# The start of a transformer block on one core: condition turned first, filler matmuls on ones, the first normalised rows on two engines

## The chip, the cores and the metric

The kernel runs on one core of a Trainium2 chip. The core has a matrix engine (TensorE, PE in the profile; its weight loads are listed as PEld), a vector engine (VectorE, DVE), a scalar engine (ScalarE, ACT), a general engine (GpSimd, POOL) and SyncE (SP), which here only issues DMAs. The metric is the device time of one execution in microseconds (us). Three runs of the kernel before took 1156.21, 1156.73 and 1157.76 us; the median is 1156.73.

## The reference

Input is x, 2 batches of 1024 tokens of width 256, one condition vector of 256 for each batch, and 77 context tokens for each batch. All weights are float32. Cut to what matters:

```python
x = x + xcond(layernorm(x), cond, ctx)
x = x + ffn(layernorm(x))              # a small network with rounded weights

def xcond(x, t, context):              # 16 heads of 64
    h1 = layernorm(x) * (1 + scale1) + shift1   # scale, shift = split(t @ norm1_w + norm1_b)
    x = mha(h1, h1) + x
    h2 = layernorm(x) * (1 + scale2) + shift2
    x = mha(h2, context) + x
    h3 = layernorm(x) * (1 + scale3) + shift3
    return glu_ff(h3) + x
```

Only the beginning concerns us: the double layer norm of the first batch's tokens, the first pair of scale and shift, and the first projections to keys and queries.

## The kernel before

All 2048 tokens lie in SBUF as 16 tiles of 128 tokens (`r_sb`). Self-attention goes unit by unit: a unit is a pair of heads with one half (512) of a batch's queries, and there are 32. A unit has 4 slots; in each slot (the loop at L1102) PE makes two groups of scores, ACT copies them out of PSUM, DVE keeps a running maximum, and the exponentials, sums on POOL and products with the values of an earlier unit are worked in between. Projections, values and other pieces are hung onto slots in three dictionaries (`pieces`, `inner`, `extras`). The order on PE, DVE, ACT and POOL in this part is the order in which the program is written, and each of these engines works strictly through its own list; a later part of the kernel is ordered by a planner, which the change doesn't touch.

Ahead of the slots stands a start of its own, written out in L1063 to L1089. PE has no weights yet. It turns the identity matrix 23 times as filler (L1066), and then turns `vec`, 32 rows of short vectors that ACT's queue has loaded: the shift vectors of three norms, the bias of the feed-forward part and the condition. ACT copies the result to `vecT` (L1068), and POOL adds one to the scale parts (L1071). DVE works out mean and variance for four tiles (`first_stats`: `bn_stats` and `bn_aggr` for each tile, then two operations on the variances), ACT takes a square root, DVE a reciprocal. The normalised rows `xn` of the first four tiles are made half by ACT, half by DVE (`first_xn`). PE multiplies condition and weights (`shift_scale_flat`), DVE copies the flat result, PE turns it into columns (`shift_scale`), and DVE adds the bias into `scsh`. `first_turned` transposes `xn` to PSUM, column half by column half, and `first_T` scales and shifts it on ACT into `h1T`, the transposed input of the projections. After that come the same steps for tiles 4 to 7, with the first halves of the k and q projections (`project`) between them, and the slots begin. `first_y` writes the normalised tokens back on POOL, which isn't waited for soon.

PSUM is handed out by tags. `two_banks` rotates two buffers of two banks, mainly for scores; `piece_bank` is one bank, `maxima_banks` a pair of banks for the broadcast maxima, which have no use for it until the second unit, and the tag `av` one bank for the products with the values. Whoever asks for a buffer waits until the readers of its last holder are done. Slot 0 has, behind its scores, the k projection of the second half of the tokens, in the maxima's banks (L1029), and slot 1 the q projection (L1030).

Loads are issued by SP in the order of L338 to L352; the queue also waits for older transfers to land.

Of the kernel before, what the change touches and what calls it, by code (L numbers as in the profile page):

```python
# [26 lines left out]
P = 128  # L27
# [16 lines left out]
def block_kernel(ctx: ExitStack, tc: tile.TileContext, a: dict, out: bass.AP):  # L44
# [20 lines left out]
    xv = a["x"].rearrange("b (t p) d -> p (b t) d", p=P)  # L65
    ident = const.tile([P, P], FP, name="ident")
# [3 lines left out]
    ones = const.tile([P, P], FP, name="ones")  # L70
    nc.gpsimd.memset(ones, 1.0)
# [194 lines left out]
    with ExitStack() as sa:  # L266
# [49 lines left out]
        for n in range(3):  # L316
            nc.scalar.dma_start(
                out=vec[4 * n : 4 * n + 4, :],
                in_=g(f"xcond_norm{n + 1}_b").rearrange("(o p) -> o p", p=P),
            )  # L320
        for c in range(DC):
            nc.scalar.dma_start(
                out=vec[28 + B * c : 28 + B * (c + 1), :],
                in_=a["cond_1024"][:, c * P : (c + 1) * P],
            )
        nc.scalar.dma_start(
            out=vec[12:28, :], in_=g("xcond_ff_b1").rearrange("(o p) -> o p", p=P)
        )
# [4 lines left out]
        def load_nw(n):  # L333
            nc.sync.dma_start(
                out=nw[n], in_=g(f"xcond_norm{n + 1}_w").rearrange("(c p) f -> p c f", p=P)
            )
# [3 lines left out]
        load_nw(0)  # L340
        load_pair(0)
        load_x(4, 4)
# [3 lines left out]
        load_pair(1)  # L346
        bo1 = load_row("xcond_attn1_bo", D)
# [218 lines left out]
        h1T, mvs, rws, xns, pts = {}, {}, {}, {}, {}  # L566

        def first_stats(b, half):
            st = small.tile([P, 4, 6], FP, tag="st4", name="st")
            mv = mvs[b, half] = p1.tile([P, 4, 2], FP, tag="mv4", name="mv", bufs=4)  # L570
            rw = rws[b, half] = p1.tile([P, 3, 4], FP, tag="rw4", name="rw", bufs=4)
            for i in range(4):
                nc.vector.bn_stats(st[:, i, :], r_sb[:, b * TB + 4 * half + i, :])
                nc.vector.bn_aggr(mv[:, i, :], st[:, i, :])
            nc.vector.tensor_scalar(rw[:, 0, :], mv[:, :, 1], 1.0 + EPS, EPS * EPS, ALU.mult, ALU.add)
            nc.vector.tensor_scalar_add(rw[:, 1, :], mv[:, :, 1], EPS)
# [16 lines left out]
        def first_xn(b, half, on_act=0):  # L593
# [4 lines left out]
            for i in range(4):  # L598
                src = r_sb[:, b * TB + 4 * half + i, :]
                if i < on_act:  # L600
                    nc.scalar.activation(
                        xn[:, i, :], src, AF.Identity,
                        bias=rw[:, 2, i : i + 1], scale=rw[:, 0, i : i + 1],
                    )
                else:
                    normed(xn[:, i, :], src, mv, rw[:, 0, :], i)

        def first_turned(b, half, parts=range(DC)):
            if b not in h1T:
                h1T[b] = hpool.tile([P, DC, S], FP, tag="hT", name=f"h1T_{b}")  # L610
            if 0 in parts:
                pts[b, half] = (maxima_banks if b else two_banks)("pt_ln")
            pt = pts[b, half]
            for c in parts:
                for i in range(4):
                    at = c * 512 + i * P
                    nc.tensor.transpose(
                        pt[:, at : at + P], xns[b, half][:, i, c * P : (c + 1) * P], ident
                    )

        def first_T(b, half):
            pt = pts.pop((b, half))
            for c in range(DC):
                nc.scalar.activation(  # L624
                    h1T[b][:, c, half * 512 : (half + 1) * 512],
                    pt[:, c * 512 : (c + 1) * 512],
                    AF.Identity,
                    bias=scsh[:, 0, 1, c, b : b + 1],
                    scale=scsh[:, 0, 0, c, b : b + 1],
                )  # L630
# [11 lines left out]
        def shift_scale_flat(n):  # L642

            pf = psx.tile([P, 512], FP, tag="av", name="pf")
            for c in range(DC):
                nc.tensor.matmul(
                    pf[:B, :],
                    lhsT=vecT[:, 28 + B * c : 28 + B * (c + 1)],
# [4 lines left out]
            if n:  # L653
                nc.scalar.copy(flat, pf[:B, :])
            else:
                nc.vector.tensor_copy(flat, pf[:B, :])

        def shift_scale(n):
# [8 lines left out]
            if n == 0:  # L667
                nc.vector.tensor_tensor(
                    scsh[:, n, :, :, :].rearrange("p s c b -> p (s c) b"),
                    pe[:, : 4 * B].rearrange("p (o b) -> p o b", b=B),  # L670
                    vecT[:, 4 * n : 4 * n + 4].unsqueeze(2).to_broadcast([P, 4, B]),
# [3 lines left out]
            for oc in range(4):  # L675
                nc.scalar.activation(
                    scsh[:, n, oc // DC, oc % DC, :], pe[:, oc * B : (oc + 1) * B], AF.Identity,
                    bias=vecT[:, 4 * n + oc : 4 * n + oc + 1],
# [383 lines left out]
        at_slot(extras, 112, load_u, 0)  # L1062
        first_stats(0, 0)  # L1063
        pv = piece_bank("pv")
        for i in range(23):
            nc.tensor.transpose(pv[:, P : 2 * P], ident, ident)  # L1066
        nc.tensor.transpose(pv[:, :NV], vec, ident[:NV, :NV])
        nc.scalar.copy(vecT, pv[:, :NV])  # L1068
        for n in range(3):
            v = vecT[:, 4 * n : 4 * n + DC]  # L1070
            nc.gpsimd.tensor_scalar_add(v, v, 1.0)  # L1071
        first_sqrt(0, 0)
        first_inverse(0, 0)
        first_xn(0, 0, 2)
        first_y(0, 0)
        shift_scale_flat(0)
        first_turned(0, 0, (0,))
        shift_scale(0)
        first_turned(0, 0, (1,))
        first_T(0, 0)  # L1080
        first_stats(0, 1)
# [4 lines left out]
        project(0, 0, "q", 0, two_banks)  # L1086
# [419 lines left out]
    with (  # L1506
# [338 lines left out]
        class Piece:  # L1845
# [25 lines left out]
            def gelu(self, f):  # L1871
# [4 lines left out]
                    bias=vecT[:, 20 + f : 21 + f],  # L1876
                )

            def gate(self, f):
                n = self.n * P  # L1880
                nc.vector.scalar_tensor_tensor(  # L1881
                    self.gT[:, f, :n], self.pu[f][:, :n], vecT[:, 12 + f : 13 + f],
# [93 lines left out]
```

## Time and profile before

| what | us |
|---|---|
| median of three runs | 1156.73 |
| the profiled execution | 1156.76 |
| its span in the trace | 1155.0 |
| PE busy | 1132.8 |
| DVE busy | 922.1 |
| POOL busy | 848.3 |
| ACT busy | 815.5 |
| first filler transpose begins | 1.45 |
| `vecT` is copied | 6.88 |
| first projection begins | 12.54 |
| second half's k projection begins | 19.85 |

The span runs from the first to the last instruction of the trace. The time of an execution is 1.76 us longer. In the lines shown below, a group of instructions has its line in the program, engine, operation, written and read tiles, the count after x, and times in us from the start of the span. "L365 PE MATMUL pp<-h1T,wk" is the projection to keys, whose helper has line 365. In the chain of work, each line is a start, a duration and what ran; in the groups, busy time and mean nanoseconds stand behind the first bar, idle time ahead of it and who ended it behind the second.

### The profile page before, as it was taken

The numbers are of one execution on the slowest core, as the hardware profiler recorded it, in microseconds if no ns is written. First come the engines' busy times: TensorE is split into PE (matmuls) and PEld (weight loads), VectorE is DVE, ScalarE is ACT, GpSimd is POOL, SyncE is SP. The second block draws the span as 40 slices with busy tenths as digits, with TensorE's granted clock in tenths as the row PEclk, the third lists the DMA queues.
The fourth block names the chain that finished last, engine by engine and source line by source line (L and its number), as shares of the span: only waits on it lengthen the run. The fifth ranks groups of instructions, "written<-read, shape, count | busy, mean of one in ns | idle before, by whom it ended". The sixth has DMA issues, their size and how long they took to land.

```text
span 1155.0 us, 18728 instructions
## 1 busy us (share of the span) xinstructions
PE 1132.8 (98%) x6964; PEld 531.9 (46%) x6964; DVE 922.1 (80%) x1319; ACT 815.5 (71%) x1023; POOL 848.3 (73%) x654
## 2 busy tenths in 40 slices
PE   8999999999999999999999999999999999999997
PEld 4333333333333333333333333355677866486685
DVE  5898889879888988989987899977767634587497
ACT  4788887888887888888889888765544231665366
POOL 5688989888888788888988899979765424424145
PEclk9999999999999999999999999999999999999999
DMA  7011212212122121211113212121201020000000
GB/s 242 25 33 56 72 60 67 69 50 81 48 74 61 57 79 38 85 51 61 56 40 103 95 38 83 34 92 43 82 1 74 1 82 19 1 19 10 10 10 29
DMA packets 65041, 64.32 MB, mean 56 GB/s; under 512 B 23675, under 2 KB 54709, under 8 KB 64309
## 3 DMA queue, kind: packets, MB, share of 16 engines
q1 hardware_dynamic: 64885, 63.10, 17.5%
q8 instruction: 55, 0.90, 0.3%
q14 instruction: 37, 0.30, 0.1%
q10 hardware_dynamic: 64, 0.02, 0.0%
HBM read 55.36 MB, written 7.73 MB: 55 GB/s over the span
## 4 chain that ended last, share of the span: by engine, by line
PE 82%; DVE 10%; ACT 5%; issue 2%; POOL 1%; DVEq 0%; ACTq 0%; POOLq 0%
PE sc L432 17%; PE pav L506 16%; PE pu L1863 10%; PE pp L365 9%; PE po L948 6%; PE po L1889 5%; PE sc L859 4%; PE pv L365 4%; PE po L365 3%; DVE macc L448 3%; DVE sT L488 3%; ACT sT L1107 2%; ACT sT L491 2%; PE tot L529 1%; POOL pacc L498 1%
## 5 line engine op out<-in xcount | busy, mean ns | idle before, releaser
L498 POOL TENSOR_TENSOR pacc<-pacc,sT 128x1024 f32<-128x1024 f32 x192 | 457.1, 2381 | 25.8 <-ACT sT L491 15.5
L448 DVE TENSOR_TENSOR macc<-macc,sc 128x1024 f32<-128x1024 f32 x192 | 233.8, 1218 | 71.1 <-ACT sT L1107 59.5
L1107 ACT COPY sT<-sc 128x1024 f32<-128x1024 f32 x256 | 248.0, 1017 | 51.8 <-PE sc L432 51.6
L491 ACT ACTIVATE sT<-sT 128x1024 f32<-128x1024 f32 x256 | 260.1, 1064 | 13.3 <-DVE sT L488 11.8
L488 DVE TENSOR_TENSOR sT<-sT,mb 128x1024 f32<-128x1024 f32 x224 | 260.0, 1205 | 3.5 <-ACT mb L479 3.4
L432 PE MATMUL sc<-qT,kT 64*64 64x512 f32 x2048 | 252.9, 604 | 3.4 <-DVE macc L448 1.9
L506 PE MATMUL pav<-sT,v 128*64 128x512 f32 x1024 | 248.5, 605 | 2.9 <-ACT sT L491 2.4
L506 PEld LDWEIGHTS pav<-sT,v 128*64 128x64 f32 x1024 | 61.6, 136 | 160.0 <-issue 72.0
L432 PEld LDWEIGHTS sc<-qT,kT 64*64 64x64 f32 x2048 | 62.7, 131 | 150.1 <-issue 59.8
L498 POOL TENSOR_TENSOR pacc<-sT 128x1024 f32<-128x1024 f32 x32 | 76.3, 2384 | 67.0 <-ACT sT L491 66.9
L1863 PE MATMUL pu<-h2T,ffw 128*128 128x512 f32 (+1 forms) x320 | 114.0, 508 | 0.0
L1863 PEld LDWEIGHTS pu<-h2T,ffw 128*128 128x128 f32 x320 | 59.7, 190 | 44.8 <-issue 41.1
L484 POOL TENSOR_TENSOR sT<-sT,wide 128x1024 f32<-128x1024 f32 x32 | 76.2, 2380 | 1.7 <-DMA wide<-md 1.7
L859 PE MATMUL sc<-h1T,G 128*128 128x512 f32 x160 | 72.0, 602 | 0.0
L948 PE MATMUL po<-U,p 128*128 128x256 f32 x320 | 71.4, 380 | 0.0
L1881 DVE SCALAR_TENSOR_TENSOR gT<-pu,vecT,ge 128x512 f32<-128x512 f32 (+1 forms) x40 | 25.7, 641 | 50.2 <-ACT ge L1874 50.1
L948 PEld LDWEIGHTS po<-U,p 128*128 128x128 f32 x320 | 59.9, 190 | 8.0 <-issue 0.2
L365 PE MATMUL pv<-wv,h1T 128*64 128x256 f32 x512 | 61.8, 379 | 0.0
L365 PE MATMUL po<-wo,aT 128*64 128x256 f32 x512 | 61.5, 380 | 0.3 <-POOL aT L562 0.3
L365 PE MATMUL pp<-h1T,wk 128*64 128x512 f32 x256 | 60.6, 594 | 0.9 <-ACT h1T L624 0.9
L365 PE MATMUL pp<-h1T,wq 128*64 128x512 f32 x256 | 60.5, 593 | 0.0
L1874 ACT ACTIVATE ge<-pu,vecT 128x512 f32<-128x512 f32 (+1 forms) x40 | 23.9, 598 | 50.0 <-PE pu L1863 50.0
(195 smaller groups left out, 1491.6 us busy)
## 6 DMA issues: line engine op xcount, KB each, us to landing
wide<-md SPq DMA_DIRECT2D x32, 512.0 KB
rinv<-td SPq DMA_DIRECT2D x64, 128.0 KB
ffw<-in_L_xcond_ff_w_dram SPq DMA_DIRECT2D x3, 1024.0 KB
gd<-cw SPq DMA_DIRECT2D x32, 80.0 KB
ud<-cw SPq DMA_DIRECT2D x32, 80.0 KB
U<-ud SPq DMA_DIRECT2D x2, 1280.0 KB
wk<-in_L_xcond_attn_wk_dram SPq DMA_DIRECT2D x16, 128.0 KB
wq<-in_L_xcond_attn_wq_dram SPq DMA_DIRECT2D x16, 128.0 KB
```

The lines of the kernel that those rows point to most:

```text
L365: nc.tensor.matmul(dst[half, :], lhsT=lhsT[:, half], rhs=rhs, start=start, stop=stop)
L432: nc.tensor.matmul(sc[cols, j * 512 : (j + 1) * 512], lhsT=kTs[b, pair][rows, kb * P + c * DH : kb * P + (c + 1) * DH], rhs=qTs[b, pair][r ...
L448: nc.vector.tensor_tensor(maccs[u], old, sc, ALU.max)
L484: nc.gpsimd.tensor_tensor(t, t, wides[u], ALU.subtract)
L488: nc.vector.tensor_tensor(sT[u, kb], sT[u, kb], mbs[u], ALU.subtract)
L491: nc.scalar.activation(sT[u, kb], sT[u, kb], AF.Exp)
L498: nc.gpsimd.tensor_tensor(paccs[u], old, sT[u, kb], ALU.add)
L506: nc.tensor.matmul(pavs[u][j * DH : (j + 1) * DH, :], lhsT=vs[b, pair // 2][:, kb, at : at + DH], rhs=sT[u, kb][:, j * 512 : (j + 1) * 512 ...
L859: nc.tensor.matmul(sc[:, j * 512 : (j + 1) * 512], lhsT=Gs[self.b][c][:, 2 * k + j, :], rhs=hT[:, c, self.at : self.at + 512], start=(c == 0),
L948: nc.tensor.matmul(self.po[i][:, :D], lhsT=self.t[piece // 2][:, at : at + P], rhs=Us[self.b][:, piece, :], start=(piece == 0), stop=(piec ...
L1107: nc.scalar.copy(sT[v, kb], sc)
L1863: nc.tensor.matmul(pu[:, k * 512 : k * 512 + n], lhsT=ffw1[c][:, at : at + P], rhs=hT[:, c, at0 : at0 + n], start=(c == 0), stop=(c == DC ...
```

## The change

The vectors in `vec` change places: the condition comes first, then the shift vectors, then the feed-forward bias. Only the condition and the first shift vector are loaded by ACT's queue; the others go to SP's, behind the second pair of projection weights. The first 8 rows are turned and copied alone, the other 24 in slot 1 (`later_vectors`). The weights of the first scale and shift are loaded in two pieces, and tiles 4 to 7 in two. The tile of ones is filled by DVE instead of POOL, at the head of the program.

The 23 transposes of the identity become 15 matmuls of ones (128 x 128) with 64 columns of ones, the turning of 8 vectors, and 8 more such matmuls, into a pair of banks of `two_banks`. The product of condition and weights moves ahead of the normalised rows, its copy from DVE to ACT. All four tiles of `xn` are made by DVE. The eight transposes go tile by tile, two tiles to each of two PSUM buffers, and `first_T` reads one buffer on ACT and the other on DVE. The moments of tiles 4 and 5 are taken between `xn` and `scsh`, those of 6 and 7 after `first_T`. The second half's transposes take the maxima's banks instead of `two_banks`, and the first q projection the bank of tag `av`.

```diff
...
     r_sb = const.tile([P, NT, D], FP, name="r_sb")
     xv = a["x"].rearrange("b (t p) d -> p (b t) d", p=P)
+    ones = const.tile([P, P], FP, name="ones")
+    nc.vector.memset(ones, 1.0)
     ident = const.tile([P, P], FP, name="ident")
     make_identity(nc, ident)
     ident_bf = const.tile([P, P], BF, name="ident_bf")
     nc.vector.tensor_copy(ident_bf, ident)
-    ones = const.tile([P, P], FP, name="ones")
-    nc.gpsimd.memset(ones, 1.0)
     NV = 32
     vecT = const.tile([P, NV], FP, name="vecT")
     scsh = const.tile([P, 3, 2, DC, B], FP, name="scsh")
...
         nw12 = w8.tile([P, 2, DC, 2 * D], FP, tag="aT", name="nw12")
         nw = [nw0, nw12[:, 0, :, :], nw12[:, 1, :, :]]
         ctx_sb = w8.tile([CTX, B, D], FP, tag="aT", name="ctx_sb")
-        for n in range(3):
-            nc.scalar.dma_start(
-                out=vec[4 * n : 4 * n + 4, :],
-                in_=g(f"xcond_norm{n + 1}_b").rearrange("(o p) -> o p", p=P),
-            )
         for c in range(DC):
             nc.scalar.dma_start(
-                out=vec[28 + B * c : 28 + B * (c + 1), :],
-                in_=a["cond_1024"][:, c * P : (c + 1) * P],
-            )
-        nc.scalar.dma_start(
-            out=vec[12:28, :], in_=g("xcond_ff_b1").rearrange("(o p) -> o p", p=P)
-        )
+                out=vec[B * c : B * (c + 1), :], in_=a["cond_1024"][:, c * P : (c + 1) * P]
+            )
+
+        def load_shift(n, queue):
+            queue.dma_start(
+                out=vec[4 + 4 * n : 8 + 4 * n, :],
+                in_=g(f"xcond_norm{n + 1}_b").rearrange("(o p) -> o p", p=P),
+            )
+
+        load_shift(0, nc.scalar)
         def load_x(t, n):
             nc.sync.dma_start(out=r_sb[:, t : t + n, :], in_=xv[:, t : t + n, :])
-        def load_nw(n):
+        def load_nw(n, parts=slice(0, DC)):
             nc.sync.dma_start(
-                out=nw[n], in_=g(f"xcond_norm{n + 1}_w").rearrange("(c p) f -> p c f", p=P)
+                out=nw[n][:, parts, :],
+                in_=g(f"xcond_norm{n + 1}_w").rearrange("(c p) f -> p c f", p=P)[:, parts, :],
             )
         load_x(0, 2)
         load_x(2, 2)
-        load_nw(0)
+        for c in range(DC):
+            load_nw(0, slice(c, c + 1))
+        load_x(4, 2)
         load_pair(0)
-        load_x(4, 4)
+        load_x(6, 2)
         load_wv(0)
         load_x(8, 4)
         load_x(12, 4)
         load_pair(1)
+        load_shift(1, nc.sync)
+        load_shift(2, nc.sync)
+        nc.sync.dma_start(
+            out=vec[16:NV, :], in_=g("xcond_ff_b1").rearrange("(o p) -> o p", p=P)
+        )
         bo1 = load_row("xcond_attn1_bo", D)
         load_nw(1)
         load_nw(2)
...
-        h1T, mvs, rws, xns, pts = {}, {}, {}, {}, {}
+        h1T, sts, mvs, rws, xns, pts = {}, {}, {}, {}, {}, {}
         def first_stats(b, half):
-            st = small.tile([P, 4, 6], FP, tag="st4", name="st")
-            mv = mvs[b, half] = p1.tile([P, 4, 2], FP, tag="mv4", name="mv", bufs=4)
-            rw = rws[b, half] = p1.tile([P, 3, 4], FP, tag="rw4", name="rw", bufs=4)
-            for i in range(4):
+            first_moments(b, half, range(4))
+            first_variances(b, half)
+
+        def first_moments(b, half, rows):
+            if 0 in rows:
+                sts[b, half] = small.tile([P, 4, 6], FP, tag="st4", name="st")
+                mvs[b, half] = p1.tile([P, 4, 2], FP, tag="mv4", name="mv", bufs=4)
+            st, mv = sts[b, half], mvs[b, half]
+            for i in rows:
                 nc.vector.bn_stats(st[:, i, :], r_sb[:, b * TB + 4 * half + i, :])
                 nc.vector.bn_aggr(mv[:, i, :], st[:, i, :])
+
+        def first_variances(b, half):
+            mv = mvs[b, half]
+            rw = rws[b, half] = p1.tile([P, 3, 4], FP, tag="rw4", name="rw", bufs=4)
             nc.vector.tensor_scalar(rw[:, 0, :], mv[:, :, 1], 1.0 + EPS, EPS * EPS, ALU.mult, ALU.add)
             nc.vector.tensor_scalar_add(rw[:, 1, :], mv[:, :, 1], EPS)
...
                 rw[:, 2, :], mv[:, :, 0], -1.0, rw[:, 0, :], ALU.mult, ALU.mult
             )
-        def first_xn(b, half, on_act=0):
+        def first_xn(b, half):
             xn = xns[b, half] = p3.tile([P, 1024], FP, tag="sT", name="xn").rearrange(
                 "p (i d) -> p i d", d=D
             )
             mv, rw = mvs[b, half], rws[b, half]
             for i in range(4):
                 src = r_sb[:, b * TB + 4 * half + i, :]
-                if i < on_act:
-                    nc.scalar.activation(
-                        xn[:, i, :], src, AF.Identity,
-                        bias=rw[:, 2, i : i + 1], scale=rw[:, 0, i : i + 1],
-                    )
-                else:
-                    normed(xn[:, i, :], src, mv, rw[:, 0, :], i)
+                normed(xn[:, i, :], src, mv, rw[:, 0, :], i)
         def first_turned(b, half, parts=range(DC)):
             if b not in h1T:
                 h1T[b] = hpool.tile([P, DC, S], FP, tag="hT", name=f"h1T_{b}")
             if 0 in parts:
-                pts[b, half] = (maxima_banks if b else two_banks)("pt_ln")
+                if b or half:
+                    pts[b, half] = [maxima_banks("pt_ln").rearrange("p (c n) -> p c n", c=DC)]
+                else:
+                    pts[b, half] = [
+                        two_banks("pt_ln")[:, :512].rearrange("p (c n) -> p c n", c=DC)
+                        for _ in range(2)
+                    ]
             pt = pts[b, half]
-            for c in parts:
-                for i in range(4):
-                    at = c * 512 + i * P
+            each = 4 // len(pt)
+            for i in range(4):
+                for c in parts:
                     nc.tensor.transpose(
-                        pt[:, at : at + P], xns[b, half][:, i, c * P : (c + 1) * P], ident
+                        pt[i // each][:, c, i % each * P : (i % each + 1) * P],
+                        xns[b, half][:, i, c * P : (c + 1) * P],
+                        ident,
                     )
         def first_T(b, half):
-            pt = pts.pop((b, half))
             for c in range(DC):
-                nc.scalar.activation(
-                    h1T[b][:, c, half * 512 : (half + 1) * 512],
-                    pt[:, c * 512 : (c + 1) * 512],
-                    AF.Identity,
-                    bias=scsh[:, 0, 1, c, b : b + 1],
-                    scale=scsh[:, 0, 0, c, b : b + 1],
-                )
+                for at, pt in enumerate(pts[b, half]):
+                    n = pt.shape[2]
+                    out = h1T[b][:, c, half * 512 + at * n : half * 512 + (at + 1) * n]
+                    bias, scale = scsh[:, 0, 1, c, b : b + 1], scsh[:, 0, 0, c, b : b + 1]
+                    if at:
+                        nc.vector.tensor_scalar(out, pt[:, c, :], scale, bias, ALU.mult, ALU.add)
+                    else:
+                        nc.scalar.activation(out, pt[:, c, :], AF.Identity, bias=bias, scale=scale)
         def first_y(b, half):
             for i in range(4):
...
             for c in range(DC):
                 nc.tensor.matmul(
                     pf[:B, :],
-                    lhsT=vecT[:, 28 + B * c : 28 + B * (c + 1)],
+                    lhsT=vecT[:, B * c : B * (c + 1)],
                     rhs=nw[n][:, c, :],
                     start=(c == 0),
                     stop=(c == DC - 1),
                 )
-            if n:
-                nc.scalar.copy(flat, pf[:B, :])
-            else:
-                nc.vector.tensor_copy(flat, pf[:B, :])
-
-        def shift_scale(n):
+            nc.scalar.copy(flat, pf[:B, :])
+
+        def shift_scale(n, meanwhile=lambda: None):
             pe = psx.tile([P, 512], FP, tag="av", name="pe")
             for oc in range(4):
...
                     ident[:B, :B],
                 )
             if n == 0:
+                meanwhile()
                 nc.vector.tensor_tensor(
                     scsh[:, n, :, :, :].rearrange("p s c b -> p (s c) b"),
                     pe[:, : 4 * B].rearrange("p (o b) -> p o b", b=B),
-                    vecT[:, 4 * n : 4 * n + 4].unsqueeze(2).to_broadcast([P, 4, B]),
+                    vecT[:, 4 + 4 * n : 8 + 4 * n].unsqueeze(2).to_broadcast([P, 4, B]),
                     ALU.add,
                 )
                 return
             for oc in range(4):
                 nc.scalar.activation(
                     scsh[:, n, oc // DC, oc % DC, :], pe[:, oc * B : (oc + 1) * B], AF.Identity,
-                    bias=vecT[:, 4 * n + oc : 4 * n + oc + 1],
+                    bias=vecT[:, 4 + 4 * n + oc : 5 + 4 * n + oc],
                 )
...
             at_slot(inner, 98 + 12 * half, norm_half, 1, 0, half)
         at_slot(extras, 112, load_g, 0)
         at_slot(extras, 112, load_u, 0)
+
+        def idle(times):
+            for _ in range(times):
+                nc.tensor.matmul(
+                    spare[:, :DH], lhsT=ones, rhs=ones[:, :DH], start=True, stop=True
+                )
+
+        def vectors_turned(bank, lo, hi):
+            nc.tensor.transpose(bank[:, :hi], vec[:hi, :], ident[:hi, :hi])
+            nc.scalar.copy(vecT[:, lo:hi], bank[:, lo:hi])
+            for n in range(3):
+                if lo <= 4 + 4 * n < hi:
+                    v = vecT[:, 4 + 4 * n : 4 + 4 * n + DC]
+                    nc.gpsimd.tensor_scalar_add(v, v, 1.0)
+
+        def later_vectors():
+            vectors_turned(psx.tile([P, 512], FP, tag="av", name="pv2"), 8, NV)
+
+        at_slot(inner, 1, later_vectors)
         first_stats(0, 0)
-        pv = piece_bank("pv")
-        for i in range(23):
-            nc.tensor.transpose(pv[:, P : 2 * P], ident, ident)
-        nc.tensor.transpose(pv[:, :NV], vec, ident[:NV, :NV])
-        nc.scalar.copy(vecT, pv[:, :NV])
-        for n in range(3):
-            v = vecT[:, 4 * n : 4 * n + DC]
-            nc.gpsimd.tensor_scalar_add(v, v, 1.0)
+        pv, spare = piece_bank("pv"), two_banks("spare")
+        idle(15)
+        vectors_turned(pv, 0, 8)
+        idle(8)
         first_sqrt(0, 0)
         first_inverse(0, 0)
-        first_xn(0, 0, 2)
+        shift_scale_flat(0)
+        first_xn(0, 0)
         first_y(0, 0)
-        shift_scale_flat(0)
-        first_turned(0, 0, (0,))
-        shift_scale(0)
-        first_turned(0, 0, (1,))
+        first_turned(0, 0)
+        shift_scale(0, lambda: first_moments(0, 1, (0, 1)))
         first_T(0, 0)
-        first_stats(0, 1)
+        first_moments(0, 1, (2, 3))
+        first_variances(0, 1)
         first_root(0, 1)
         first_xn(0, 1)
         first_y(0, 1)
         project(0, 0, "k", 0)
-        project(0, 0, "q", 0, two_banks)
+        project(0, 0, "q", 0, lambda name: psx.tile([P, 512], FP, tag="av", name=name))
         first_turned(0, 1)
         first_T(0, 1)
         add_row(0, TB, bo1)
...
```

In the hunk left out at the end, the feed-forward part reads its bias from the new columns of `vecT`.

## The prediction

> **What bounds the kernel now.** I read the page first: its engine table and the row of forty slices.
>
> ```profile
> PE 1132.8 (98%) x6964; PEld 531.9 (46%) x6964; DVE 922.1 (80%) x1319; ACT 815.5 (71%) x1023; POOL 848.3 (73%) x654
> ...
> PE   8999999999999999999999999999999999999997
> ```
>
> TensorE (PE) works through 39 of the 40 slices at 90% or more; only the first, 29 us long, and the last have room. The change touches only the first. After about 20 us PE has no gaps worth the name (the table of short stretches has it busy 2.00 of each 2.00 us from 20 to 30 us), so what counts is how early that unbroken stretch starts. I take its start to be the k projection of the second half of the tokens. The chain of work in order of time shows what stands ahead of it:
>
> ```profile
> 1.45 5.17 PE pv L1066 x23
> 6.62 0.24 PE pv L1067
> ...
> 7.09 1.28 ACT L584
> 8.37 0.01 issue
> 8.38 0.22 ACT rw L584
> ...
> 9.06 1.10 ACT xn L601 x2
> ...
> 11.71 0.79 ACT h1T L624
> 12.50 0.04 issue
> 12.54 3.65 PE pp L365 x16
> 16.20 1.04 PE pt_ln L617 x8
> 17.23 0.02 issue
> 17.26 1.46 ACT h1T L624 x2
> 18.71 0.04 issue
> 18.76 1.09 PE sc L432 x8
> 19.85 1.87 PE pp L365 x8
> ```
>
> So the start of the kernel hangs on the 23 filler transposes. The turned vectors come behind them, the copy of these stands ahead of the square root on ScalarE (ACT), and a table load of 1.28 us stands between copy and square root. The statistics had been ready since 6.0 us. Call E the end of the fillers: 6.41 us (in the timeline the last one starts at 6.20, and they run 0.21 apart). The DVE normalisations begin at 8.94, E + 2.53. The projections begin at P0 = 12.54, E + 6.13. The unbroken stretch begins at 19.85, P0 + 7.31.
>
> **The filler: what one costs now.** Three answers carry this: the instructions on the filler's tile, the groups of weight loads by shape, and a close look at the one place where matmuls with 128 stationary columns and almost nothing to stream follow each other.
>
> ```profile
> L1066 PE MATMUL pv<-ident x23: 421/421/477, 1.5 to 6.2; 128*128 128x128 f32 x23
> 16.13 0.86 PEld L617 LDWEIGHTS pt_ln<-ident,xn 128*128 128x128 f32 x8 [0.81 <-issue]
> L1426 PEld LDWEIGHTS pm<-wpart,ones 128*128 128x128 f32 x4 | 0.6, 191 | 0.1
> L365 PEld LDWEIGHTS pp<-h1T,wk 128*64 128x64 f32 x256 | 18.0, 137 | 37.2 <-issue 31.4 <-ACT sT L1107 3.0 <-ACT h1T L624 1.6
> L529 PEld LDWEIGHTS tot<-pacc,ones 128*32 128x32 f32 x256 | 5.0, 108 | 20.8 <-ACT sT L491 16.8 <-issue 2.1 <-POOL pacc L498 1.9
> 915.58 0.36 PE L1426 MATMUL pm<-wpart,ones 128*128 128x1 f32 x2
> 915.69 0.25 PE L1426 MATMUL pm<-wpart,ones 128*128 128x1 f32 x1
> ```
>
> 22 steps between 1.5 and 6.2 make 0.213 us per filler transpose; the same transpose at 16 us takes 0.107 (0.86 over 8). So PE ran at half speed to the end of the fillers. The first product on real weights starts at 7.12 and its four instructions take 1.88 us, exactly as those at 29.86 do, so the full clock came between 6.4 and 7.1 us, 5.0 to 5.7 us after PE's first instruction. The view's granted clock reads 1.00 throughout and does not show this. In float32 a matmul is two instructions, each with its own weight load (L1426 has four for two matmuls). The loads take 108, 137 and 191 ns for 32, 64 and 128 columns, some 0.107 us more for 128 columns than for none, and the ones that stream a single column start 0.11 us apart: there the load is the bound. One `idle` matmul loads 128 columns twice and streams 64 twice. I price it by those loads: 2 x 0.107 at full clock, 2 x 0.213 at half, twice a filler transpose of now. The other bound is the stream alone (a half of the transpose's 128 columns, twice): 0.213 at half clock. I take the loads, since L1426 has the same 128 x 128 stationary shape.
>
> **The change, part by part.** *Ones on DVE, first.* PE need no longer wait for the identity (1.41). The queues start at 0.71; POOL's fill of the same tile took 0.21; so PE starts near 0.97 instead of 1.45. If DVE is later than that, each 0.1 costs 0.1.
>
> *15 idle matmuls, then 8 vectors turned.* 30 passes from 0.97, half speed up to the time x at which the clock is released: E' = 0.97 + 30 x 0.107 + (x - 0.97)/2 = 3.69 + x/2, at most 7.37. With the delay seen now (middle 5.3 us) x = 6.3 and E' = 6.82, later than the 6.41 of now. Bounds: 4.17 (streams alone at half clock) and 7.37 (cold throughout). The Trainium skill, "TensorE: Matmul & The Clock Gate", Part 1, puts the release at 3.4 to 4 us of sustained work with a phase that isn't tied to the kernel; by it x would be 4.4 to 5.0, E' 5.9 to 6.2 and the gain below 1.2 to 0.9. Its Part 4 says that transposes don't count as work for the release, which would speak strongly for this change; the trace disagrees, since nothing but transposes came before the fast products at 7.12.
>
> *From there to the normalised rows.* The copy (8 columns instead of 32: 0.19 at most), the table load, the square root, the reciprocal and the product stay in the same order on ACT and DVE: first row E' + 2.53. All four rows go to DVE (1.46 for four, as at 14.64), so to E' + 3.99 where now two and two end at E + 3.74: 0.25 lost, and the transposes, now row by row, end at E' + 4.4. They no longer end last.
>
> *8 idle matmuls and the condition's product.* 16 passes at full clock, 1.71, from E' + 0.35; the product to E' + 3.97 (4 starts of 0.43 and 0.16 of tail); its copy on ACT, 0.6 (the copy of 128x512 takes 0.586), to E' + 4.6; four small turns, 0.45; E' + 5.05. The shift weights don't bind: SyncE's queue waited for their landing until 6.6, ahead of E' + 2.1 = 8.9. In two pieces they land no later.
>
> *DVE in the meanwhile.* Two rows' moments, 2 x 0.53, after the rows: E' + 5.05. Then `scsh`, 0.17, to about E' + 5.35 with the handover, now E + 4.96. The two chains end together, so neither half of the work is worth anything without the other.
>
> *h1T on two engines.* Now ACT starts at 11.71, 0.34 behind `scsh` (11.37), since the second four transposes end at 11.68; that wait goes, as all eight are done. ACT's 512 columns took 0.79; 256 columns, by the same start and rate, 0.58; DVE's two parts of 256 by the normalising row 0.41 each. P0' = E' + 6.02, against E + 6.13 now. Each projection half takes 0.93, so neither second part (E' + 6.45) is waited for, nor is it now.
>
> *Second half.* DVE: h1T to P0' + 0.2, two moments 1.06, variances 0.55, root 0.8 in all with the reciprocal, four rows 1.46: P0' + 4.1. The projections end at P0' + 3.65 and six of eight transposes fit in before the last row, so these end at P0' + 4.7 as now. Since they go to the maxima's banks and the q projection to the bank of the sums, both score groups have banks at once: 2 x 0.94 to P0' + 6.57, while ACT makes h1T by P0' + 6.2. The k projection follows without the stall between 18.3 and 18.76: P0' + 6.57 instead of P0 + 7.31, 0.74 gained. It needs the maxima's banks, which that same h1T frees; were ACT 0.4 later, it would be waited for. In that cover ACT's two copies of scores start at P0' + 6.25 and end 0.2 ahead of where they do now, so slot 1 gets its banks in time.
>
> *Later vectors, queues.* A turn of 0.29 at most on PE in slot 1, where nothing hides it; pipelined 0.15. ACT's copy 0.19 and POOL's two adds 0.4 lie beside it. SyncE issues five more DMAs (two pieces cut in two, three vectors taken from ACT), 0.3 to 0.5 each; what stands behind them (the first bias row, the other shift weights) is used at 20.3 and 29.9 us and was issued at 8.8 to 10.7. ACT's queue ends some 1 us earlier and its first table load with it, to no effect: it then waited 2.6 us for PE. New places of the vectors cost nothing: same reads.
>
> *Sum.* Gain = 19.85 - (E' + 6.02 + 6.57) - 0.15 = 7.11 - E'. With E' = 6.82 it is 0.3 us. The profiled execution took 1156.76 (span 1155.0, 1.76 around it), the median is 1156.73: I predict 1156.4, no measurable change, as I take 0.2% (2.3 us) to be about what can be told from none. For release between 3.4 and 7 us after the start (E' 5.9 to 7.4) it is 1155.5 to 1157.0.
>
> **Rivals.** *The filler is quick.* If passes aren't held by their loads, E' = 4.17; the square root then starts at 6.13, just behind the statistics (6.0), and the product waits for its weights (6.6 instead of 6.27, 0.3). Gain 2.7: 1154.0, faster. For it: only 64 columns stream, half a pass. Against it: the 0.11 of L1426. An early release (x = 3.5) would halve the way to it: 1155.1.
>
> *The filler doesn't open the clock (slower).* PE streams in only half of each pass, and if that isn't enough, everything to the product runs at half speed: E' = 7.37, 16 passes 3.41 to 11.1, product 3.41 to 14.7, copy, turns, sums and h1T 2.1: P0' = 16.8, 4.3 late, less 0.59 for the stall that goes and the late turn: 1160.4, and 1162.3 if the first projection is cold too. It decides by the 2.3 us only when the clock is released after some 11 us. For it: nothing in the trace has such a filler. Against it: transposes opened it.
>
> *The gain is given back.* If slot 1's scores waited for ACT's copies (the wait of scores on `macc`, 1.9 us in the whole run, is of this kind), any E' ends at 1156.7. PE's 98% speaks against it.
>
> **How the numbers follow.** Forecast 0.6, quick filler or very early release 0.2, cold filler 0.1, given back 0.1. Faster 0.2 from the quick filler; slower 0.11 from the cold one and a rest; same 0.69. The range runs from the quick filler, 1153.8, to a fully cold first group and a missed projection, 1158.0; it leaves out most of the cold rival.
>
> **What would show it.** The fillers' starts 0.21 us apart at first and 0.107 later (right), or 0.107 at first (quick filler); the first vectors' copy near 7.3; `scsh` near 12.1, the first projection near 12.8, the second half's k projection near 19.4 with no gap in front of it. If the copy comes near 5 I am wrong on the filler; if the product takes over 3 us, on the clock.

## The result, and the profile after

The changed kernel takes 1161.06 us (median of 7 runs, 1160.41 to 1161.57), the kernel before 1156.73 in the same comparison: the ratio is 1.0032, with a 95% interval from 1.0022 to 1.0041. It is 4.3 us slower. I had predicted 1156.4 with a range up to 1158.0; that was wrong. What happened is the rival to which I gave one chance in ten: the filler did not open the clock.

The profiled execution took 1160.41 us, its span is 1158.6 us. From the page of the changed kernel, the engine table's row of PE and the row of slices; then the chain of work in order of time (start, duration, what ran):

```profile
PE 1138.7 (98%) x6988; PEld 537.4 (46%) x6988; DVE 923.4 (80%) x1323; ACT 814.8 (70%) x1023; POOL 848.4 (73%) x653
...
PE   9999999999999999999999999999999999999997
```

```profile
1.03 6.67 PE spare L1082 x30
7.70 0.20 PE pv L1087
7.90 3.60 PE spare L1082 x16
11.51 3.26 PE pf L664 x4
14.77 1.03 PE pt_ln L633 x8
15.80 0.35 PE pe L677 x4
...
16.25 0.18 DVE scsh L684
...
17.09 3.65 PE pp L372 x16
20.74 1.02 PE pt_ln L633 x8
21.77 1.88 PE sc L439 x16
23.64 1.87 PE pp L372 x8
```

PE is now busy through 90% of the first slice too. That reads like an improvement and is the opposite: it is busy with filler at half speed. The last line is the k projection of the second half, which begins at 23.64 us instead of 19.85, 3.8 us late. What follows it takes 1134.96 us of the span, 1135.15 before the change, so the loss lies ahead of it; the span as a whole is 3.6 us longer. (The profiled execution is the fastest of the seven; the medians lie 4.3 us apart.)

Three answers of the same trace show the speed: the instructions on the filler's tile (duration minimum/median/maximum in ns, first and last start), the timeline, and the table of stretches, in which the third number from the end is the granted clock.

```profile
L1082 PEld LDWEIGHTS spare<-ones x46: 288/333/338, 1.0 to 11.0; 128*128 128x128 f32 x46
L1082 PE MATMUL spare<-ones x46: 421/421/475, 1.0 to 11.1; 128*128 128x64 f32 x46
```

```profile
11.44 3.33 PE L664 MATMUL pf<-nw,vecT 128*2 128x512 f32 x4
...
14.70 0.86 PEld L633 LDWEIGHTS pt_ln<-ident,xn 128*128 128x128 f32 x8 [1.47 <-issue]
```

```profile
0.00:20.00 20.00, 18.01 (x77) 12.92 (x79) 8.68 (x35) 5.33 (x9) 6.13 (x12) 1.00 0.86 264
```

The 30 loads before the first vectors take 6.48 us and the 16 behind them 3.49, some 0.216 us a pass in both groups, so none was quicker towards the end. Then the product takes 3.33 us instead of 1.88, its starts 0.81 to 0.85 apart instead of 0.43. At 14.70 the transposes come 0.107 apart. So the clock stayed at half speed for 13 us and was released some 3 us into the product, which streams all the time, though only two stationary columns of the array are in use. The view's granted clock reads 1.00 over all of this, as it did before the change.

How much of a pass is streaming follows from the same numbers. At half clock 512 columns take 0.85 us, so a column takes 1.67 ns, and 64 columns take 0.107 us: half of the 0.213 us between two starts, which the load of 128 columns sets. In the same way 80 columns fill 0.63 of it, 96 three quarters, and 128 all of it.

### The profile page after: what moved, and what is told of

It is laid out like the page before. It is cut to its first block, busy times and chain, and to the rows that moved or that the text cites. A ratio compares the mean times of both kernels' runs of the same rounds, so it can differ in the third digit from the quotient of the medians.

```text
span 1158.6 us, 18786 instructions
## 1 busy us (share of the span) xinstructions
PE 1138.7 (98%) x6988; PEld 537.4 (46%) x6988; DVE 923.4 (80%) x1323; ACT 814.8 (70%) x1023; POOL 848.4 (73%) x653
## 4 chain that ended last, share of the span: by engine, by line
PE 82%; DVE 10%; ACT 5%; issue 2%; POOL 1%; DVEq 0%; ACTq 0%; POOLq 0%
PE sc L439 17%; PE pav L513 16%; PE pu L1894 10%; PE pp L372 8%; PE po L964 6%; PE po L1920 5%; PE sc L875 4%; PE pv L372 4%; PE po L372 3%; DVE macc L455 3%; DVE sT L495 3%; ACT sT L1138 2%; ACT sT L498 2%; PE tot L536 1%; POOL pacc L505 1%
## 5 line engine op out<-in xcount | busy, mean ns | idle before, releaser
L505 POOL TENSOR_TENSOR pacc<-pacc,sT 128x1024 f32<-128x1024 f32 x192 | 457.1, 2381 | 25.0 <-ACT sT L498 14.7
```

The costliest lines, as they stand in the source:

```text
L505: nc.gpsimd.tensor_tensor(paccs[u], old, sT[u, kb], ALU.add)
```

## The experiments

Three theories stood at the start. *S*: what releases the clock is the share of time in which PE streams columns, and a pass that loads 128 columns and streams 64 has too little of it. *D*: it is the data, because ones with ones switch nothing. *O*: the order is to blame (the product ahead of the rows, its copy on ACT), and the clock is beside the point.

**Stream 128 columns instead of 64.** The pass is held by its load, so it lasts as long as before.

```diff
-                    spare[:, :DH], lhsT=ones, rhs=ones[:, :DH], start=True, stop=True
+                    spare[:, :P], lhsT=ones, rhs=ones[:, :P], start=True, stop=True
```

> One edit to the changed kernel: each filler matmul streams 128 columns of ones instead of 64. By the 0.107 us that a load of 128 columns takes, a pass lasts as long as before (0.21 us at half clock), only PE streams through all of it instead of half. Theory S (what releases the clock is the share of time in which PE streams; 64 columns fill half of a pass that its load holds up): the passes fall from 0.21 to 0.107 us apart some 5.0 to 5.7 us after the first, first 15 over at 6.8 to 7.2, the product's four starts 0.43 apart, second half's k projection at 19.4 to 19.8 instead of 23.64, time 1156 to 1157. Theory D (the data: ones next to ones switch nothing, and that doesn't count): half clock to the product as before, time 1160.4 to 1161.6. Theory O (the loss is in the new order, product ahead of the rows and its copy on ACT, not in the clock): even if the passes speed up, the k projection comes after 22 us and the time stays above 1159.

Measured: 1156.19 us, ratio to the kernel before 0.9993 (0.9984 to 1.0002). The chain of this variant:

```profile
1.03 6.12 PE spare L1082 x30
7.15 0.15 PE pv L1087
7.30 1.98 PE spare L1082 x16
9.29 1.81 PE pf L664 x4
11.10 1.02 PE pt_ln L633 x8
12.12 0.35 PE pe L677 x4
...
13.41 3.65 PE pp L372 x16
17.07 1.02 PE pt_ln L633 x8
18.09 1.88 PE sc L439 x16
19.97 1.87 PE pp L372 x8
```

The last passes of the first group are already fast (30 take 6.12 us, not 6.67), the second group takes 1.98 instead of 3.60, the product 1.81 instead of 3.26. Nothing but the number of streamed columns is different, and all of the loss is gone. D and O fall here: the ones are the same, and so is the order. The time is also the one that I had forecast for an open clock (1156.4).

**The identity instead of ones, 64 columns.**

```diff
-                    spare[:, :DH], lhsT=ones, rhs=ones[:, :DH], start=True, stop=True
+                    spare[:, :DH], lhsT=ident, rhs=ident[:, :DH], start=True, stop=True
```

> One edit to the changed kernel: the filler matmuls take the identity for both operands (the data of the 23 transposes of before), still 64 columns. PE starts some 0.3 us later, behind the identity. Theory S: 0.21 us a pass to the end, product's starts 0.82 apart, 1160.5 to 1162. Theory D: the clock is released 5.0 to 5.7 us after the first pass, product's starts 0.43 apart, 1156 to 1157.5. Theory O: above 1159 either way.

Measured: 1160.61 us (ratio 1.0033, 1.0021 to 1.0046), the filler at half speed throughout. The first group in its chain, as slow as that of the ones (6.67):

```profile
1.34 6.66 PE spare L1082 x30
```

The identity had opened the clock before the change, as a transpose of 128 columns; with 64 columns it doesn't.

**Halve the load instead of doubling the stream.** 64 stationary columns, 64 streamed, twice as many matmuls.

```diff
-                    spare[:, :DH], lhsT=ones, rhs=ones[:, :DH], start=True, stop=True
+                    spare[:DH, :DH], lhsT=ones[:, :DH], rhs=ones[:, :DH], start=True, stop=True
...
-        idle(15)
+        idle(30)
...
-        idle(8)
+        idle(16)
```

> The changed kernel with the loads of its filler halved instead of the stream doubled: 64 columns of ones stationary, 64 streamed, and twice as many matmuls (30 and 16). A pass then loads for 0.107 us and streams for 0.107 at half clock: as many columns in each matmul as in the changed kernel, as much time in all, but PE streams throughout. Theory S (share of time streamed): clock released 4.5 to 6 us after the first pass, product's four starts 0.43 apart, second half's k projection at 19.4 to 20, time 1156 to 1157. Theory C (a matmul of 64 columns is too short to count, whatever the share; or each load breaks the work): half clock up to the product, starts 0.82 to 0.85 apart, 1160.4 to 1161.6.

Measured: 1155.99 us (ratio 0.9992, 0.9983 to 1.0001). From its timeline:

```profile
1.03 5.05 PEld L1082 LDWEIGHTS spare<-ones 128*64 128x64 f32 x60 [1.03 <-DVE ones L67]
...
8.32 1.88 PE L664 MATMUL pf<-nw,vecT 128*2 128x512 f32 x4
```

60 passes in 5.05 us are some 32 that start 0.107 apart and the rest 0.058: the clock came about 3.3 us after the first pass. These matmuls stream as few columns as those of the changed kernel, and there are more loads than before, so theory C of the expectation falls: neither the length of a matmul nor a load in between matters. What differs is the share of time streamed.

**Where the bound lies.** 96 and 80 columns against the same load, three quarters and 0.63 of a pass.

```diff
-                    spare[:, :DH], lhsT=ones, rhs=ones[:, :DH], start=True, stop=True
+                    spare[:, :96], lhsT=ones, rhs=ones[:, :96], start=True, stop=True
```

> The changed kernel with 96 columns streamed by each filler matmul: the pass is still as long as its load (0.213 us at half clock), PE streams through three quarters of it. Theory S says only that the bound lies between half (no release in 10 us) and the whole (release after 3.5 to 5.7 us). Release before the product: time 1156 to 1157, product's starts 0.43 apart, the bound is below three quarters. None: 1160.4 to 1161.6, and it is above.

> The same with 80 columns, PE streams through 0.63 of each pass. Release before the product: 1156 to 1157; none: 1160.4 to 1161.6. If 96 columns don't release the clock, these don't either.

Measured: 1156.70 us with 96 columns, 1160.94 with 80. The first group of the filler in the timeline, of the variant with 96 and of that with 80:

```profile
1.03 5.31 PEld L1082 LDWEIGHTS spare<-ones 128*128 128x128 f32 x30 [1.03 <-DVE ones L67]
```

```profile
1.03 6.48 PEld L1082 LDWEIGHTS spare<-ones 128*128 128x128 f32 x30 [1.03 <-DVE ones L67]
...
7.86 3.49 PEld L1082 LDWEIGHTS spare<-ones 128*128 128x128 f32 x16
```

With 96 columns the release comes about 4.1 us after the start, with 80 not within 10. For fillers of this kind the bound lies between 0.63 and 0.75 of the time. One of the eight runs with 96 took 1160.64 us, just the time of a closed clock; no trace was kept of it, so whether 96 is near the edge stays open.

**The filler of the kernel before, exchanged alone.**

```diff
-        for i in range(23):
-            nc.tensor.transpose(pv[:, P : 2 * P], ident, ident)
+        for i in range(12):
+            nc.tensor.matmul(
+                pv[:, P : P + DH], lhsT=ones, rhs=ones[:, :DH], start=True, stop=True
+            )
```

> One edit to the kernel before: its 23 transposes (4.9 us) become 12 matmuls of ones with 64 columns, 24 passes of 0.21 us (5.1 us), all else as before the change. Theories S and D: clock not released at the product, whose four starts lie 0.82 apart instead of 0.43 (1.6 us, of which all but some 0.4 lies beside the rows), the transposes behind it and perhaps the first projection at half clock (up to 1.9 us more): 1157.2 to 1159.5. Theory O: product at full clock as before, 1156.2 to 1157.2.

Measured: 1157.37 us (ratio 1.0006, 0.9997 to 1.0015). The clock stayed closed here too, as the product in the timeline shows:

```profile
7.02 3.57 PE L646 MATMUL pf<-nw,vecT 128*2 128x512 f32 x4 [0.28 <-ACT vecT L1070]
```

It took 1.88 us before the change. But the span is only 0.6 us longer, and the interval does not tell the times apart. In the old order nearly all of a slow product lies beside the table load, the square root and the rows, and the product itself opened the clock in time for the projections. So a closed clock costs some 0.6 us in the old order and 4.9 in the new one (1161.06 against the 1156.19 with 128 columns): the new order has 46 passes ahead of the product, where this variant has 24. One of the ten runs here took 1160.67 us; it has no trace, so its cause stays open (a release only in the projections is one that would fit).

**No filler at all.**

```diff
-        idle(15)
         vectors_turned(pv, 0, 8)
-        idle(8)
```

> The changed kernel without its fillers; vectors turned as soon as they land, rows from 6.6 to 8.1. If the fillers of the changed kernel do nothing but take time: product from 6.3 at half clock, 3.4 us, to 9.8, the rest behind it at half or full clock, first projection near 12 to 13.5, time 1155.5 to 1158, thus well below the changed kernel's 1161. If they had still brought the release nearer, so that without them it comes only in the projections or later, 1158 to 1162.

Measured: 1156.32 us (ratio 0.9991, 0.9982 to 1.0000), 4.7 us less than with the filler that the changed kernel has. From the timeline:

```profile
4.38 0.18 PEld L1087 LDWEIGHTS pv<-ident,vec 8*128 8x128 f32 x1 [4.38 <-issue]
...
6.36 3.57 PE L664 MATMUL pf<-nw,vecT 128*2 128x512 f32 x4 [1.71 <-DMA nw<-in_L_xcond_norm_w_dram]
...
9.86 0.96 PEld L633 LDWEIGHTS pt_ln<-ident,xn 128*128 128x128 f32 x8 [1.71 <-DVE mv L586]
```

The product begins when its weights land, at 6.36, and runs at half speed to its end; the release comes with the first of the transposes behind it, some 3.7 us after the product's start. With the 46 passes ahead of it the product begins 5.1 us later, and the release comes some 4.4 us later (3.0 us after the product's start). So the filler brought no early release; whether it shortened the product's own part can't be told, since behind the other half-speed fillers that part is 1.9 us (identity), 3.7 (the kernel before) and 4.0 (80 columns).

**Transposes as filler in the new order.** Each idle matmul becomes one transpose of the identity.

```diff
-                nc.tensor.matmul(
-                    spare[:, :DH], lhsT=ones, rhs=ones[:, :DH], start=True, stop=True
-                )
+                nc.tensor.transpose(spare[:, :P], ident, ident)
```

> One edit to the changed kernel: each filler matmul of two passes becomes one transpose of the identity, as before the change; 15 ahead of the first vectors, 8 behind, all else as in the changed kernel. Start 1.33, 15 at 0.213: first vectors turned near 4.6, square root near 6.4, right behind the statistics; rows 6.9 to 8.4; product from 6.6 when its weights land. Theories S and D: the clock is released between 6.3 and 7.0, first projection near 10.5, second half's k projection near 17.0, time 1153.5 to 1155; if the release comes a window of 3.4 us later (fewer fillers in all), the product's starts are 0.82 apart, and it is 1155 to 1157. Theory O: above 1158.

Measured: 1154.28 us, ratio 0.9978 (0.9969 to 0.9987): faster than both kernels, and what the rest of the change is worth. Its chain:

```profile
1.34 3.46 PE spare L1082 x15
4.81 0.20 PE pv L1085
5.01 1.58 PE spare L1082 x8
6.59 1.81 PE pf L664 x4
8.40 1.02 PE pt_ln L633 x8
9.42 0.35 PE pe L677 x4
...
10.72 3.65 PE pp L372 x16
14.37 1.02 PE pt_ln L633 x8
15.39 1.88 PE sc L439 x16
17.27 1.87 PE pp L372 x8
```

The vectors are turned 1.8 us earlier than before the change, so most of the table load lies beside the statistics, and the projections begin at 10.72 instead of 12.54.

**The banks of the second half, undone on that variant.**

```diff
-                    pts[b, half] = [maxima_banks("pt_ln").rearrange("p (c n) -> p c n", c=DC)]
+                    bank = maxima_banks if b else two_banks
+                    pts[b, half] = [bank("pt_ln").rearrange("p (c n) -> p c n", c=DC)]
...
-        project(0, 0, "q", 0, lambda name: psx.tile([P, 512], FP, tag="av", name=name))
+        project(0, 0, "q", 0, two_banks)
```

> On the variant with 15 and 8 transposes as filler (1154.28 us, k projection of the second half 6.55 us after the first projection) the second half's transposes and the first q projection go back to the score buffers, as before the change. As predicted for the banks: the second score group waits for ACT's second half again, the k projection comes 7.2 to 7.4 us after the first projection, and the time is 0.6 to 0.9 above that variant, 1154.9 to 1155.3. Rival: the wait that is saved comes back in slot 1 (ACT's copies of the scores), and the two take the same time, 1154.1 to 1154.5.

Measured: 1154.97 us (ratio 0.9979, 0.9970 to 0.9988). That is 0.7 above the variant with the maxima's banks, but the two were not run side by side, and against the kernel before the ratios are the same (0.9978 there). So the times show nothing of the banks; the chain shows the term by itself:

```profile
11.36 3.65 PE pp L372 x16
15.01 1.04 PE pt_ln L634 x8
16.05 0.03 issue
16.07 1.46 ACT h1T L649 x2
17.53 0.04 issue
17.57 1.09 PE sc L439 x8
18.66 1.87 PE pp L372 x8
```

From the first projection to the k projection of the second half it takes 7.30 us, with the maxima's banks 6.55: 0.75. (The projections start later here, at 11.36, because the second piece of the weights landed late in this execution: PE waited 1.0 us for it between the two halves of the product. In this execution a part of the longer time is that wait; whether other runs had it too isn't known, so the time may have met its forecast by luck.)

**h1T on ACT alone, on the variant with transposes.**

```diff
-                    pts[b, half] = [
-                        two_banks("pt_ln")[:, :512].rearrange("p (c n) -> p c n", c=DC)
-                        for _ in range(2)
-                    ]
+                    pts[b, half] = [two_banks("pt_ln").rearrange("p (c n) -> p c n", c=DC)]
```

> On the variant with 15 and 8 transposes (1154.28 us, first projection 0.64 us after the first h1T instruction) the first h1T goes back to ACT alone, two instructions of 512 columns from one score buffer. As predicted: 0.79 instead of 0.57 until the first projection starts, 0.2 later, 1154.3 to 1154.7; DVE is then free 1 us earlier for the second half's rows, which are not waited for. Rival: the second part, ready 1.45 us after the first instruction's start, holds up the projection too: 0.4 to 0.7 later, 1154.7 to 1155.

Measured: 1154.63 us (ratio 0.9982, 0.9973 to 0.9991), again not run beside the variant it is held against. In its trace the first projection starts 0.83 us behind the first h1T instruction, with two engines 0.65. The 0.18 is what was predicted; the second part holds nothing up. In time the two variants can't be told apart.

**Small turns between the transposes, 128 columns, 7 and 5 fillers.** An attempt at a faster version.

```diff
-        idle(15)
+        idle(7)
         vectors_turned(pv, 0, 8)
-        idle(8)
+        idle(5)
...
-        first_turned(0, 0)
-        shift_scale(0, lambda: first_moments(0, 1, (0, 1)))
+        first_turned(0, 0, (0, 1))
+        shift_scale(0, lambda: (first_turned(0, 0, (2, 3)), first_moments(0, 1, (0, 1))))
```

> The changed kernel with fillers of 128 columns of ones, 7 ahead of the first vectors and 5 behind (24 passes, some 5 us in all, from 1.03 us), and the condition's four small turns put between the first four and the last four of the first transposes, so that they wait for their copy and not for all eight. Theory S and the chain read from the trace of the variant with 15 and 8 transposes (product 6.52, transposes 8.33, small turns 9.35, first projection 10.72): product from 6.2 to 6.5, small turns 0.3 earlier behind it, first projection near 10.1 to 10.4, time 1153.4 to 1154.2. If 24 passes are too few for the clock, the product's starts are 0.82 apart and the time is 1155 to 1156.5.

Measured: 1154.40 us (ratio 0.9974, 0.9963 to 0.9984), no better than the variant with transposes. From its timeline:

```profile
6.91 1.88 PE L664 MATMUL pf<-nw,vecT 128*2 128x512 f32 x4 [0.48 <-DMA nw<-in_L_xcond_norm_w_dram]
...
9.97 0.17 DVE L684 TENSOR_TENSOR scsh<-pe,vecT 128x8 f32<-128x8 f32 x1 [0.40 <-PE pe L677]
10.18 1.02 ACT L648 ACTIVATE h1T<-pt_ln,scsh 128x256 f32<-128x256 f32 x2 [0.78 <-DVE scsh L684]
10.49 0.99 DVE L646 TENSOR_SCALAR h1T<-pt_ln,scsh 128x256 f32<-128x256 f32 x2 [0.35 <-PE pt_ln L633]
```

The first projection begins at 11.13, not at 10.1 to 10.4: both hopes met a new wait. The filler ends earlier, but the product waits for its weights until 6.91. And `scsh` comes 3.06 us behind the product's start instead of 3.35, but now DVE's share of h1T waits 0.35 for the four transposes that were put back.

## Why the prediction was wrong

**The step that failed** is the second one, *15 idle matmuls, then 8 vectors turned*: "With the delay seen now (middle 5.3 us) x = 6.3 and E' = 6.82". I carried the delay of the transposes over to a filler of another kind. The clock did not come within the 10.4 us of filler at all, and E' was 7.51. The product, which was to take 1.88 us, took 3.33: the sign that I had set for being wrong on the clock (over 3 us). Of the 4.25 us by which the first projection is later than predicted (17.09 against 12.84), 0.7 lie ahead of E', 1.9 in the 16 passes behind the first vectors, and 1.7 from the product on. The price of a pass was right (0.213 predicted from its load, and 0.213 between starts as measured), and the reason for which it was right is the reason for which the clock stayed closed: a pass that is held up by its load streams for half of its time. I had that number in hand, as the ground of the slow rival, and weighed it with 0.1 because "transposes opened it". The transposes stream through their whole pass (128 columns at 1.67 ns are the 0.213 us between their starts); they were no evidence on this filler.

**The slow rival** was right in its mechanism and near in its numbers: E' 7.37 against 7.51, the product over at 14.7 against 14.77, first projection 16.8 against 17.09, 1160.4 us against 1161.06. The projections were not slow, as its second figure had them. The range ended below it. With two outcomes 4 us apart and no row for the new filler, the range should have held both.

**The clock rule.** The Trainium skill, "TensorE: Matmul & The Clock Gate", Part 1, has the release after about 3.4 us of sustained work, with a phase that isn't tied to the kernel. The runs are near that where the filler streams: 2.8 to 5.3 us after the first pass. The three variants with 15 and 8 transposes have the same program up to the release and differ all the same: 4.8, 3.5 and 2.8 us, the last of them below the page's figure (the eight transposes behind the vectors load in 1.42, 0.86 and 0.86 us, the fifteen ahead of them in 3.06, 3.06 and 2.96). The runs show in addition that, in these float32 fillers, work counts as sustained only above a share of streaming between 0.63 and 0.75. Part 4 there says that transposes don't count in the same way; 23 of them opened the clock before the change, and 15 and 8 do so in the fastest variant.

**From the filler to the projections**, P0' = E' + 6.02: with an open clock it was 6.46 (128 columns: the last pass ends near 6.95, the projection starts at 13.41). The term that was too small is "the transposes, now row by row, end at E' + 4.4". PE is in the product until E' + 4.1, so the eight transposes run in one block behind it and the four small turns behind that block: they start at 12.04, E' + 5.1, not E' + 4.6. The sum itself could have told: it has the product end at E' + 3.97, and eight transposes of 0.107 behind it end at E' + 4.83 at the earliest.

**h1T on two engines** gave 0.18 to the first projection; predicted were 0.2 (0.58 instead of 0.79).

**The second half**: 0.74 predicted, 0.75 in the trace with these banks undone; the distance was 6.57 by the sum and is 6.55 to 6.56 in the traces with an open clock.

**A misread row**: the page before the change has 38 of the 40 slices at 90% or more, not 39; the first shows 8 and the last 7. Nothing in the sum rests on it.

**Ones on DVE**: first pass at 1.03, predicted 0.97. **Queues and later vectors** cost nothing that shows beyond the 0.17 of the turn in slot 1, predicted 0.15.

**The sum** for an open clock, 1156.4, met the 1156.19 of the filler with 128 columns partly by luck. The k projection of the second half was to begin at 19.41 (6.82 + 6.02 + 6.57) and began at 19.97, later than the 19.85 of before the change. What follows it took 1134.93 us of the span instead of 1135.15, where the sum had 0.15 more for the turn; where these 0.2 come from, no run shows. So with that filler the new order gains next to nothing, since the filler ends later than the old one. Of the 2.5 us by which the variant with transposes beats the kernel before, 0.75 are the banks' and 0.2 h1T's, by the distances in the traces; the rest, by subtraction, I put down to turning the vectors early. The transposes get there in half the time of the matmuls on ones, and open the clock besides.

## What to carry to other kernels

A filler that is to open the clock has to stream, not just to occupy the engine: compare the load and the stream of one pass, and take one whose stream fills it. The busy row and the granted clock of the profile don't tell; the distance between starts of equal instructions does. And a filler has a price of its own: where they left the clock at half speed, 46 passes cost 4.7 us more than having none.

## What the runs showed of the hardware

- A PE that is busy all the time can stay at half speed. 10.4 us of float32 matmuls with 128 x 128 stationary, back to back but for one small turn, left the clock there with 64 or 80 streamed columns (0.5 and 0.63 of the time); 96 and 128 columns, and 64 columns against a load of 64, released it 3.3 to 5.3 us after the first pass.
- Two stationary columns are enough: with no filler ahead of it, the product of condition and weights (128 x 2 stationary, 512 streamed) released it by itself, some 3.7 us after its start.
- Constant data opens it too (128 columns of ones with ones), and the identity does not where only 64 columns are streamed.
